# A selective-scan hybrid network on one core: every fourth scan unit takes its input product from GpSimd

## The chip, the cores and the metric

The kernel runs on 1 core of one Trainium2 chip. The metric is the device time of one execution in microseconds (us). Three executions of the kernel before took 7193.72, 7199.61 and 7202.72 us, so the median is 7199.61 us. The five engines of the core are called PE (TensorE), DVE (VectorE), ACT (ScalarE), POOL (GpSimd) and SP (SyncE, which here only issues DMAs). Each has its own queue of instructions and works it off in order.

## The reference

Four images of 1024 positions and 256 channels go through four layers: a convolution and selective-scan block (layer 0, 64 states), a bottleneck convolution (layer 1), graph attention and a mixture of experts (layer 2), and a second selective-scan block with 16 states and another mixture of experts (layer 3). The part that the change touches is the scan. For every channel `d` and state `n` it computes, along the positions:

```python
def step(h, inp):
    xt, dtt, Bt, Ct = inp
    dA = jnp.exp(dtt[:, :, None] * A)
    h = dA * h + (dtt * xt)[:, :, None] * Bt[:, None, :]
    y = jnp.einsum('bdn,bn->bd', h, Ct)
    return (h, y)
```

There are 512 channels, so layer 0 has 512 x 64 such recurrences for each image and layer 3 has 512 x 16.

## The kernel before, in words

**Units.** One unit is a 128 x 1024 f32 tile: 128 recurrences (2 channels with 64 states, or 8 channels with 16 states) on the partitions, 1024 positions along the row. `scans` (L336) lists 1280 of them. The order of the eight scans is fixed by `SCANS` (L31): images 0, 1, 2 of layer 0 (units 0 to 767), images 0 and 1 of layer 3 (768 to 895), image 3 of layer 0 (896 to 1151), and images 2 and 3 of layer 3 (1152 to 1279).

**What a unit does.** `load` (L382) has SP broadcast the rows of `dt` from DRAM over the states into a tile `dA`: two DMAs of 256 KB in layer 0, eight of 64 KB in layer 3. It is called three units ahead, and `dA` has four buffers. `first` (L397), one unit ahead, has PE repeat `dt*u` over the states with two bf16 matmuls into the PSUM tile `ps_rep` (two buffers), and has ACT turn `dA` into the decay exp(A dt) in place. DVE then multiplies `ps_rep` by the row tile of B in place and runs the recurrence with `tensor_tensor_scan` into `h` (five buffers). POOL multiplies `h` by the row tile of C. `pair` (L415) has PE sum two units over the states into `ps_y`.

**What stands beside the units.** All other work belongs to stages (`STAGES`, L33): `front` of an image (what comes before scan 0), `middle` (what follows scan 0 up to the inputs of the image's layer 3 scan: layer 1, attention, experts and `front3`), and `last` (after scan 3: the second expert layer and the output). `front(0)` runs before the first unit and `last(3)` after the last one. The other stages are generators that yield after each small step, and `run` (L490) calls such steps between the units.

**What sets the order.** The scans and the stages run under a manual schedule: instructions stand in each engine's queue in the order in which `run` emits them. `run` keeps a planner's clock for each engine. A wrapper (`Metered`, L88) adds to it a fixed cost for every instruction: for GpSimd's `tensor_tensor` 2.3 us for 1000 columns plus 0.06, for VectorE's 1.18 plus 0.06, for the scan 2.23. After each half of a unit, `run` lets stages advance by at most two steps, and only as long as no clock is ahead of VectorE's:

```python
now = clock["vector"]
for e in clock:
    clock[e] = max(clock[e], now - LAG)
for _ in range(TICKS):
    if max(clock.values()) > clock["vector"] + LEAD or self.advance() is None:
        break
```

`LEAD` is 0, `LAG` is 4 us and `TICKS` is 2. Stages start in the order of `STAGES`, one at a time, as soon as the scan that they wait for is done.

**Where the order is forced.** Twelve units (`AHEAD`) before a scan begins, `chunk` (L356) calls `need` (L465). If the stage that prepares this scan is not finished, `need` advances stages until it is, with no unit in between, and sets all the clocks to the latest one. After the last unit, `run` works off what is left of the stages. In the kernel before, one long stretch is forced: most of `middle(3)`, before the scan of image 3 of layer 3.

**Scatter.** Between the first 64 units POOL also issues one indirect DMA for each unit (`scatter`, L975), which builds the attention mask.

**`steps`** (L527), called at the end of `front` and of `front3`, computes `dt` and `dt*u`, writes `dt` to DRAM, splits `dt*u` into three bf16 parts for PE's repetition, and writes these to DRAM as well. It works on eight items of 128 x 512, with four POOL instructions for each.

Of the kernel before, what the change touches and what calls it, by code (L numbers as in the profile page):

```python
# [7 lines left out]
F32 = mybir.dt.float32  # L8
BF16 = mybir.dt.bfloat16
I32 = mybir.dt.int32  # L10
AF = mybir.ActivationFunctionType
ALU = mybir.AluOpType
# [4 lines left out]
P = 128  # L17
NB = 4
L = 1024
# [16 lines left out]
    ("last", 1, (3, 1)), ("last", 2, (3, 2)),  # L36
)
SAFE = 40.0
AHEAD = 12


# [83 lines left out]
class Hybrid:  # L125
# [41 lines left out]
    def pipe(self, items, *steps, cost=1.0):  # L167

        items = list(items)
        for tick in range(len(items) + len(steps) - 1):  # L170
            for s in reversed(range(len(steps))):
                if 0 <= tick - s < len(items):
                    steps[s](items[tick - s])
            yield cost if tick < len(items) else 0.5
# [126 lines left out]
    def scan_setup(self, stage, psum, name, n):  # L301
# [18 lines left out]
        for s in range(3):  # L320
# [6 lines left out]
        nc.vector.tensor_reduce(  # L327
            mine, self.ident.rearrange("p (g n) -> p g n", n=n), AX.X, ALU.add
        )
# [6 lines left out]
    def scans(self, mp, psum):  # L336

        nc = self.nc
        units = []
        for scan in SCANS:
            G = P // self.states[scan[0]]
            units += [
                (scan, d, c, i, j)
                for d in range(DC) for c in range(2) for i in range(32 // G) for j in range(2)  # L350
            ]
        chunks, rows = {}, {}
        state = {}
        y = None

        def chunk(k):  # L356

            if k >= len(units):
                return
            scan, d, c, i, j = units[k]  # L360
            if (c, i, j) != (0, 0, 0):
                return
            n = self.states[scan[0]]
            if d == 0:
                self.need(scan)
                bct = self.mem["bc", *scan]
                pair = []
                for t in range(2):
                    x = mp.tile([P, L], F32, tag=f"rows{t}", name=f"rows{t}", bufs=2)
                    for g in range(P // n):  # L370
                        nc.sync.dma_start(x[g * n : (g + 1) * n, :], bct[t * n : (t + 1) * n, :])
                    pair.append(x)
                rows[scan] = pair
            S = mp.tile([3 * 32, 4, L], BF16, tag="S", name="S", bufs=2)
            for s in range(3):
                nc.sync.dma_start(
                    S[32 * s : 32 * s + 32, :, :],
                    self.mem["parts", *scan, d][s].rearrange("(j p) t -> p j t", p=32),
                )
            chunks[scan, d] = S  # L380

        def load(k):  # L382
            if k >= len(units):
                return
            scan, d, c, i, j = units[k]
            n = self.states[scan[0]]
            G = P // n
            a = mp.tile([P, L], F32, tag="dA", name="dA", bufs=4)
            for g in range(G):
                r = 64 * c + 32 * j + G * i + g  # L390
                nc.sync.dma_start(
                    a[g * n : (g + 1) * n, :],
                    self.mem["dt", *scan, d][r : r + 1, :].to_broadcast([n, L]),
                )
            state[k] = a

        def first(k):  # L397
            if k >= len(units):
                return
            scan, d, c, i, j = units[k]  # L400
            A, spread, _ = self.tables[scan[0]]
            G = P // self.states[scan[0]]
            ps = psum.tile([P, L], F32, tag="x", name="ps_rep", bufs=2)
            for g in range(2):
                cols = slice(g * 512, (g + 1) * 512)
                nc.tensor.matmul(
                    ps[:, cols], lhsT=spread[:, i, :], rhs=chunks[scan, d][:, 2 * c + j, cols],
                    start=True, stop=True,
                )
            a = state.pop(k)  # L410
            col = (d * P + 64 * c + 32 * j) // G + i
            nc.scalar.activation(a, a, AF.Exp, scale=A[:, col : col + 1])
            state[k] = (a, ps)

        def pair(k):  # L415

            nonlocal y
            scan, d, c, i, j = units[k]
            n = self.states[scan[0]]
            per = 32 * n // P  # L420
            collect = self.tables[scan[0]][2]
            if i == 0:
                y = psum.tile([P, 512], F32, tag="y", name="ps_y", bufs=1)
            h = [state.pop(k - 1), state.pop(k)]
            for g in range(2):
                for j in range(2):
                    at = 32 * (2 * g + j)
                    nc.tensor.matmul(
                        y[at : at + 32, :], lhsT=collect[:, i, :],
                        rhs=h[j][:, g * 512 : (g + 1) * 512],  # L430
                        start=(i == 0), stop=(i == per - 1), tile_position=(0, at),
                    )
            if i == per - 1:
                yo = mp.tile([P, 512], F32, tag="yo", name="yo", bufs=2)
                nc.scalar.copy(yo, y)
                to = self.keep(("y", *scan, d, c), [64, L])
                for g in range(2):
                    nc.sync.dma_start(to[:, g * 512 : (g + 1) * 512], yo[64 * g : 64 * g + 64, :])
                if d == DC - 1 and c == 1:
                    self.done.add(scan)  # L440

        for k in range(AHEAD):
            chunk(k)
        for k in range(3):
            load(k)
        first(0)
        for k in range(len(units) + 4):
            chunk(k + AHEAD)
            load(k + 3)
            first(k + 1)  # L450
            if k < len(units):
                a, inp = state.pop(k)
                B, Cm = rows[units[k][0]]
                nc.vector.tensor_tensor(inp, inp, B, ALU.mult)
            yield
            if k < len(units):
                h = mp.tile([P, L], F32, tag="h", name="h", bufs=5)
                nc.vector.tensor_tensor_scan(h, a, inp, 0.0, ALU.mult, ALU.add)
                nc.gpsimd.tensor_tensor(h, h, Cm, ALU.mult)
                state[k] = h  # L460
            if k % 2 == 1 and 2 <= k < len(units) + 2:
                pair(k - 2)
            yield
# [63 lines left out]
    def steps(self, fp, key, w, src, chunks, bias, u):  # L527


        nc = self.nc  # L530
        for d in range(DC):
            self.keep(("dt", *key, d), [P, L])
            self.keep(("parts", *key, d), [3, P, L], BF16)
        got = {}

        def tile2(tag, bufs):
            return fp.tile([P, 512], F32, tag="sp_" + tag, name="sp_" + tag, bufs=bufs)
# [23 lines left out]
        def split(item):  # L561
            d, g = item
            r, _, _, x = got[item]
            nc.sync.dma_start(self.mem["dt", *key, d][:, g * 512 : (g + 1) * 512], r)
            X = fp.tile([P, 3, 512], BF16, tag="parts", name="parts", bufs=3)
            rest = tile2("x", 2)
            nc.scalar.copy(X[:, 0, :], x)
            nc.vector.tensor_tensor(rest, x, X[:, 0, :], ALU.subtract)
            nc.scalar.copy(X[:, 1, :], rest)
            got[item] = rest, X  # L570

        def low(item):
            rest, X = got[item]
            nc.gpsimd.tensor_tensor(X[:, 2, :], rest, X[:, 1, :], ALU.subtract)

        def store(item):
# [7 lines left out]

        yield from self.pipe(
            [(d, g) for d in range(DC) for g in range(2)], project, add, split, low, store, cost=3.0
        )

# [517 lines left out]
    def shift(self, fp, qT, kT, mT):  # L1106
# [28 lines left out]

        nc.vector.tensor_scalar(most[:, 0:1], most[:, 0:1], SAFE * SAFE, None, ALU.is_lt)
        nc.vector.tensor_scalar(most[:, 0:1], most[:, 0:1], -1.0, 1.0, ALU.mult, ALU.add)
# [583 lines left out]
```

## Time and profile before

| what | value |
|---|---|
| median of 3 executions | 7199.61 us |
| the profiled execution | 7197.44 us, of which the profile's span is 7195.7 us |
| DVE busy | 5221.8 us (73%) |
| PE busy | 5436.2 us (76%) |
| POOL busy | 3649.9 us (51%) |
| ACT busy | 3287.1 us (46%) |
| first scan starts, last scan ends | 317.9 us, 6780.2 us |
| DMA | 939.01 MB, mean 130 GB/s |

The profile is of one execution; its own time is 1.7 us more than its span. A busy share is a mean over stretches of very different kinds, so the stretches have to be told apart: before the first scan, while units run, the one stretch in which a stage is forced and no unit runs, and after the last scan. A line that names L120 is of the wrapper that meters instructions; its tile name tells what it is: `h<-dA,ps_rep` is the scan, `ps_rep<-ps_rep,rows` the product with B, `h<-h,rows` the product with C, `dA<-dA` the decay.

### The profile page before, as it was taken

How to read it: one execution, taken by the hardware profiler on the slowest of the kernel's cores; microseconds unless marked ns; L12 is line 12 of the kernel's file. 1: busy time of each engine (PE TensorE's matmuls, PEld its weight loads, DVE VectorE, ACT ScalarE, POOL GpSimd, SP SyncE). 2: the span in 40 equal slices, each digit the busy share in tenths (PEclk: the TensorE clock that was granted, in tenths of full speed). 3: DMA queues.
4: the chain of work that ended last, by engine and by line, in shares of the span. 5: the costliest groups of instructions: out<-in, count | busy, mean ns of one | idle time of the engine just before them, and what ended most of it. 6: DMA issues, size and time to landing. Idle time of an engine off the chain costs nothing. (4 is left out here: it accounts for less than half of the span.)

```text
span 7195.7 us, 66163 instructions
## 1 busy us (share of the span) xinstructions
PE 5436.2 (76%) x20431; PEld 2208.0 (31%) x20516; DVE 5221.8 (73%) x4477; ACT 3287.1 (46%) x4024; POOL 3649.9 (51%) x1801
## 2 busy tenths in 40 slices
PE   7185876578798568879557889859889777866979
PEld 3020221132242022234113224315444322523556
DVE  2888898878898987889887778889888710237611
ACT  4164665234466334456523446636556332243411
POOL 1287677555557655545755455665555510045300
PEclk8585876579898578979657888969989889876989
DMA  2356665654455664446565545666656610135421
GB/s 81 79 141 163 162 176 161 168 136 120 112 153 159 163 160 125 119 121 174 150 169 133 131 123 143 171 166 159 181 137 164 167 40 1 48 96 154 120 62 32
DMA packets 395051, 939.01 MB, mean 130 GB/s; under 512 B 83268, under 2 KB 165776, under 8 KB 393040
## 3 DMA queue, kind: packets, MB, share of 16 engines
q1 hardware_dynamic: 392512, 932.10, 48.8%
q8 instruction: 172, 2.82, 0.2%
q0 software_dynamic: 2128, 2.13, 0.2%
q14 instruction: 239, 1.96, 0.1%
HBM read 844.17 MB, written 93.95 MB: 130 GB/s over the span
## 5 line engine op out<-in xcount | busy, mean ns | idle before, releaser
L120 POOL TENSOR_TENSOR h<-h,rows 128x1024 f32<-128x1024 f32 x1280 | 3025.5, 2366 | 2208.9 <-DVE h L120 2019.3
L120 DVE TENSOR_TENSOR_SCAN h<-dA,ps_rep 128x1024 f32<-128x1024 f32 x1280 | 2925.2, 2285 | 342.1 <-ACT dA L120 122.3
L120 DVE TENSOR_TENSOR ps_rep<-ps_rep,rows 128x1024 f32<-128x1024 f32 x1280 | 1551.8, 1212 | 270.8 <-PE ps_rep L120 254.5
L120 ACT ACTIVATE dA<-dA,A_L_conv_A_log 128x1024 f32<-128x1024 f32 x1024 | 1156.4, 1146 | 972.4 <-DMA dA<-dt 815.2
L120 PE MATMUL ps_rep<-S,spread_L_conv_A_log 96*128 96x512 bf16 x2048 | 779.2, 471 | 995.8 <-DVE h L120 796.7
L120 PE MATMUL ps_y<-h,collect_L_conv_A_log 128*32 128x512 f32 x4096 | 768.8, 771 | 88.0 <-POOL h L120 84.2
L120 PEld LDWEIGHTS <-spread_L_conv_A_log 96*128 96x128 bf16 x2048 | 159.3, 104 | 1817.3 <-DVE h L120 1370.2
L120 PE MATMUL ps_h<-xTm,we 128*128 128x512 f32 x1280 | 597.9, 611 | 26.0 <-ACT h_m L120 26.0
L120 PE MATMUL ps_e<-we,h_m 128*128 128x256 f32 x2560 | 591.8, 383 | 10.7 <-ACT h_m L120 8.4
L120 ACT ACTIVATE p<-ps_sc 128x512 f32<-128x512 f32 x512 | 277.8, 594 | 580.3 <-PE ps_sc L120 423.5
L120 ACT ACT_TABLE_LOAD x356 | 456.7, 1283 | 184.7 <-DMA dA<-dt 126.1
L120 PEld LDWEIGHTS ps_e<-we,h_m 128*128 128x128 f32 x2560 | 484.3, 191 | 136.8 <-issue 24.8
L120 ACT ACTIVATE dA<-dA,A_L_attn_A_log 128x1024 f32<-128x1024 f32 x256 | 292.5, 1148 | 415.3 <-DMA dA<-dt 380.0
L120 PE MATMUL ps_at<-p,v 128*32 128x512 f32 x1024 | 364.4, 630 | 66.1 <-ACT p L120 58.1
L120 PE MATMUL ps_rep<-S,spread_L_attn_A_log 96*128 96x512 bf16 x512 | 186.9, 453 | 220.9 <-DVE h L120 195.8
L120 PEld LDWEIGHTS ps_h<-xTm,we 128*128 128x128 f32 x1280 | 247.0, 196 | 312.7 <-issue 241.1
L120 ACT ACTIVATE h_m<-ps_h,cols 128x512 f32<-128x512 f32 x320 | 209.6, 685 | 278.0 <-PE ps_h L120 276.6
L120 DVE SCALAR_TENSOR_TENSOR tb<-ps_e,cw,tb 128x256 f32<-128x256 f32 x448 | 192.5, 473 | 191.0 <-PE ps_e L120 190.3
L120 PE MATMUL ps_sc<-qT,kT 32*128 32x512 f32 x1024 | 304.2, 669 | 7.9 <-issue 7.9
L120 PE MATMUL ps_at<-p,ones 128*32 128x512 f32 x1024 | 281.5, 630 | 0.0
L120 DVE RECIPROCAL sums<-sums 128x512 f32<-128x512 f32 x16 | 53.6, 3353 | 303.3 <-ACT sums L120 303.3
L120 PEld LDWEIGHTS ps_y<-h,collect_L_conv_A_log 128*32 128x32 f32 x4096 | 98.1, 120 | 444.6 <-issue 225.8
(406 smaller groups left out, 5695.2 us busy)
## 6 DMA issues: line engine op xcount, KB each, us to landing
dA<-dt SPq DMA_DIRECT2D x2048, 256.0 KB
dA<-dt SPq DMA_DIRECT2D x2048, 64.0 KB
we<-in_L_ffn_W_dram SPq DMA_DIRECT2D x64, 512.0 KB
parts<-parts SPq DMA_DIRECT2D x64, 384.0 KB
S<-parts SPq DMA_DIRECT2D x96, 256.0 KB
dt<-sp_r SPq DMA_DIRECT2D x64, 256.0 KB
y<-yo SPq DMA_DIRECT2D x128, 128.0 KB
y_back<-y SPq DMA_DIRECT2D x64, 256.0 KB
```

What stands on the lines that cost most here:

```text
L120: return got(*args, **kw)
```

## The change

For every fourth unit (the last of each four, `pooled`), four things differ. The values of `dt*u` are also written to DRAM (`dtu`, in `steps`). SP broadcasts their rows over the states into a new SBUF tile `inp` with two buffers (`early`, called five units ahead, with as many DMAs as `load` has). POOL multiplies `inp` by B (`product`, called two units ahead), in place of PE's two matmuls and DVE's product. ACT writes the decay into the PSUM tile in place of `dA`, so that the scan again reads one operand from PSUM and one from SBUF. The other three of four units are as before.

```diff
+TURN = 4
...
-        state = {}
+        state, given = {}, {}
...
+        def pooled(k):
+            return k % TURN == TURN - 1
+
+        def early(k):
+
+            if k >= len(units) or not pooled(k):
+                return
+            scan, d, c, i, j = units[k]
+            n = self.states[scan[0]]
+            G = P // n
+            inp = mp.tile([P, L], F32, tag="inp", name="inp", bufs=2)
+            for g in range(G):
+                r = 64 * c + 32 * j + G * i + g
+                nc.sync.dma_start(
+                    inp[g * n : (g + 1) * n, :],
+                    self.mem["dtu", *scan, d][r : r + 1, :].to_broadcast([n, L]),
+                )
+            given[k] = inp
+
+        def product(k):
+            if k < len(units) and pooled(k):
+                inp = given[k]
+                nc.gpsimd.tensor_tensor(inp, inp, rows[units[k][0]][0], ALU.mult)
+
...
+            if pooled(k):
+                col = (d * P + 64 * c + 32 * j) // G + i
+                nc.scalar.activation(ps, state.pop(k), AF.Exp, scale=A[:, col : col + 1])
+                state[k] = (ps, given.pop(k))
+                return
...
+        for k in range(5):
+            early(k)
...
             chunk(k + AHEAD)
+            early(k + 5)
             load(k + 3)
+            product(k + 2)
             first(k + 1)
...
-                nc.vector.tensor_tensor(inp, inp, B, ALU.mult)
+                if not pooled(k):
+                    nc.vector.tensor_tensor(inp, inp, B, ALU.mult)
...
+            self.keep(("dtu", *key, d), [P, L])
...
+            nc.sync.dma_start(self.mem["dtu", *key, d][:, g * 512 : (g + 1) * 512], x)
```

The planner's constants are left as they are. Its clocks count the new POOL product and no longer count the removed DVE product and PE matmuls.

## The prediction

> **What bounds the kernel now.** I read the table of stretches first: the busy time of each engine from the span's start, in the order PE, PEld, DVE, ACT, POOL, then the granted clock, the DMA share and GB/s.
>
> ```profile
> 1213.00:1384.00 171.00, 93.93 (x288) 11.15 (x288) 160.90 (x96) 53.78 (x48) 111.09 (x48) 0.50 0.63 161
> 318.00:5786.00 5468.00, 4180.26 (x16015) 1569.11 (x16084) 4636.23 (x3565) 2750.02 (x3253) 3316.94 (x1598) 0.79 0.57 151
> 5786.00:6409.00 623.00, 496.39 (x1862) 215.51 (x1877) 83.14 (x196) 202.56 (x334) 70.75 (x57) 0.90 0.09 29
> 6409.00:6780.00 371.00, 257.65 (x956) 115.80 (x955) 286.75 (x229) 163.72 (x171) 191.91 (x88) 0.75 0.59 153
> 6780.00:7195.00 415.00, 372.03 (x1316) 252.16 (x1312) 58.65 (x150) 75.66 (x114) 17.08 (x13) 0.93 0.16 48
> ```
>
> Row 1 holds units with nothing beside them: DVE is busy 160.90 of 171 us, so there it is the bound. Row 3 is the forced middle(3): PE works alone and DVE has 83 of 623 us. Row 5 is the end of last(2) and all of last(3). The units, rows 2 and 4, take 5468 + 371 = 5839 us. Then the costliest groups, and DVE in a stretch without side work:
>
> ```profile
> L120 POOL TENSOR_TENSOR h<-h,rows 128x1024 f32<-128x1024 f32 x1280 | 3025.5, 2366 | 2208.9 <-DVE h L120 2019.3
> L120 DVE TENSOR_TENSOR_SCAN h<-dA,ps_rep 128x1024 f32<-128x1024 f32 x1280 | 2925.2, 2285 | 342.1 <-ACT dA L120 122.3
> L120 DVE TENSOR_TENSOR ps_rep<-ps_rep,rows 128x1024 f32<-128x1024 f32 x1280 | 1551.8, 1212 | 270.8 <-PE ps_rep L120 254.5
> ```
>
> ```profile
> 2402.61 2.29 DVE L120 TENSOR_TENSOR_SCAN h<-dA,ps_rep 128x1024 f32<-128x1024 f32 x1 [0.19 <-issue]
> 2404.81 1.21 DVE L120 TENSOR_TENSOR ps_rep<-ps_rep,rows 128x1024 f32<-128x1024 f32 x1
> 2406.21 2.29 DVE L120 TENSOR_TENSOR_SCAN h<-dA,ps_rep 128x1024 f32<-128x1024 f32 x1 [0.19 <-issue]
> ```
>
> A unit alone takes 2406.21 - 2402.61 = 3.60 us. With side work the mean is 5839/1280 = 4.56 us. So 5839 - 1280 x 3.60 = 1231 us of the units' time is what the side work adds, and in return it hides nearly all of front(1) to last(1).
>
> **Local effect of the change.** Four units now hold three products on DVE, not four. A pooled scan starts when the one before it ends, so four units take 3 x 3.60 + 2.3 = 13.1 us on DVE, or 3.28 a unit, not 3.60. POOL gets five instructions of 2.366 where it had four, 11.8 of 13.1 us. ACT's exponential keeps its 1.15 us (at half this length ACT's rows take 602 ns into PSUM and 597 to 630 into SBUF). PE loses 640 of 2560 bf16 matmuls of 0.46 us, about 300 us spread over all the units. The pooled scan is not in this trace. It has one operand in each memory, as now, so I take 2.285 us; I see nothing that makes it shorter, and the upper end is the factor by which DVE's product of 1024 columns grows when all is in SBUF (y_back 1665 against 1212 ns): 0.85 x 320 = 270 us.
>
> New waits: ACT's exponential of a pooled unit waits until the scan two units back frees the PSUM tile, and ACT's side work queues behind it. That scan ends 3.5 us before the result is needed, and PE's matmuls wait at this place now. POOL's product waits for the `inp` transfer, issued three units earlier, and the C product of the unit before queues behind it; POOL is then 1.1 us late, catches up within four units, and `h` has five buffers. I cost both at nothing in bare units; where front's POOL work comes between, it is in the pace that I take below.
>
> Alone this is 320 x 1.3 = 416 us less. It can't be had as it stands, because **the planner moves the side work**. By its own costs four units are 3 x (1.27 + 2.28) + 2.28 = 12.94 us on VectorE and 5 x 2.415 = 12.08 us on GpSimd. That leaves 0.215 us of GpSimd a unit for stages, or 275 us in 1280 units; before it was 3.55 - 2.415 = 1.14 us a unit. What the stages want of POOL is 3650 busy less 3026 for h, less 65 for the scatter, 45 in front(0) and 15 in last(3): 500 us. The 64 scatter DMAs, at 1.0 us each, come first and eat the room of some 300 units. So about half the side work finds no place beside the units. It is then forced by `need`, or left to the end, where nothing hides it. The order in which the built program's instructions stand says the same and gives the places. Before, only middle(3) (ahead of unit 1204) is forced. Now five things stand with no unit between them: all of front(1) before unit 244; 104 of 128 expert matmul entries and front3 of middle(0) before unit 756; middle(1) from its attention on before 820; all of last(0) but its start and all of middle(3) before 1204; and the experts of last(1), all of last(2) and last(3) after the last unit.
>
> **Forced stretches, by what the same work took alone in this trace.** front(0) from its first statistics (37.6 us) to its last store (209.4) took 172: front(1) 175. In row 3 the experts took 6161 to 6274, front3 6274 to 6410: 104/128 x 113 + 136 = 228. Middle(1) lacks 22 us of row 3's 623: 600. last(3) ran 6893 to 7189, 296 us; last(0) has its first 25 us done, 272; middle(3) is row 3's 623 and back0 with layer 1, which I put at 110 from their instructions (between 80 and 135): 1005 together. Sum **2008 us, where 623 stood**. The tail: last(1) from its experts' routing 250, last(2) 296, last(3) 296 and 3 of turnover: **845 where 415 stood**.
>
> **Units.** Stretches, with the pace of each:
> - 0 to 64: POOL is the bound. 5/4 x 2.366 + 1.01 (indirect DMA) = 3.97, and 4.57 with the 0.6 that each of these waited: 4.4 x 64 = 280.
> - 64 to 244, bare: 3.28 and 0.04 of margin: 3.32 x 180 = 598.
> - 244 to 568, front(2) and front(3) thinly spread: now 62 units with a front take 34 to 39 us over 3.60 each; POOL is near its limit, so I take 3.61: 1170.
> - 568 to 756, back0, layer 1 and attention of middle(0): attention is PE's (4.84 a unit now, 4.5 with fewer matmuls): 780.
> - 820 to 1204: 896 to 1152 hold middle(2), 4.07 a unit, 1042; its layer 3 units stand in the next line.
> - 756 to 820 and all other layer 3 units are **SP's**:
>
> ```profile
> 6736.84 14.93 SPq L391 DMA_DIRECT2D dA<-dt  x32
> ```
>
> 32 issues in 14.93 us are 0.467 each: 8 a unit 3.73 us, already at DVE's pace; with `early` 10 a unit, 4.7. These are 285 (756 to 820), 357 and 244 (820 to 896, 1152 to 1204), and 357 (1204 to 1280).
>
> Units together: 280 + 598 + 1170 + 780 + 1042 + 285 + 357 + 244 + 357 = 5113, that is **726 less than 5839**. DMA: five transfers of 512 KB in 13.1 us are 200 GB/s. This row shows a burst for one unit:
>
> ```profile
> 2402.40:2404.40 2.00, 1.85 (x8) 0.12 (x8) 1.81 (x2) 1.15 (x1) 1.40 (x1) 0.50 0.90 246
> ```
>
> So 246 GB/s is had, and loads are issued about 10 us before their scan and land in 4.6. I cost them at nothing; if 181 GB/s, the highest slice of the page, were the limit, a bare unit would take 3.62.
>
> The Trainium skill ("SBUF — State Buffer", section "Door 1: The DMA port swizzle") speaks against this: 64 partitions reach only 8 of 16 ports, 196 GB/s, and two such transfers at once gain 6%. By it five transfers would take 12.6 to 13.4 us, level with DVE, and the sum would grow by up to 60 us. The 246 GB/s above are over its figure, so the row is taken.
>
> The `dtu` stores (64 issues of about 0.4 us on SP, mostly where SP is idle) and one `early` ahead of the first load cost 4 us at the start: 322. The sum is 322 + 5113 + 2008 + 845 = 8288 us for the profiled execution; its 7197.44 us stands 2 us below the median, so **8290 us**, 15% slower.
>
> **Rivals.**
> - DVE's freed time decides and the order costs nothing: 7197 - 416 = 6780, faster. For it: DVE's 160.90 of 171 us. Against: the forced stretches hold none of the pooled work. It decides only if they shrink to today's 623. 2%; no change at all 1%.
> - The same order, but units nearer their floors: layer 3 units at 3.3 since SP catches up in the forced stretches (-1.4 x 250 = -350), fronts at 3.4 (-70), middle(2) at 3.7 (-95): 7775. 12%.
> - Transfers or POOL bound all bare units: +0.34 x 830 = 280, or scans slower out of PSUM, +270: 8570, both 8840. 15%.
> - My forecast: 70%.
>
> Slower in 97, faster by over 0.2% in 2, within it in 1 of 100 (0.2% is about what a measurement of this kernel can tell from no change). The range, 7960 to 8600, takes in the unknown sizes of back0, of POOL's waits (50 us each) and of the pace under side work (0.25 us on 900 units), half of the way to the lower rival and the upper one's single price.
>
> **What would show it.** DVE's longest gaps ahead of scans 244, 756, 820 and 1204, of about 175, 230, 600 and 1000 us; three expert stages after the last scan; POOL's group of 320 products at 2.37 us; bare units at 13.1 us for four; layer 3 units at 4.7 with SP issuing without a break. It is wrong if those gaps are filled with scans, if a pooled scan takes over 2.4 us, or if DVE waits for POOL's product or the `inp` transfer in the bare units.

## The result and the profile after

The kernel with the change takes **8502.96 us** (median of four executions, 8495.25 to 8509.75), the kernel before 7200.54 us (four executions). The ratio is 1.181, with a 95% interval of 1.179 to 1.183. The prediction was 8290 us in a range of 7960 to 8600: the direction and the range hold, and the prediction is 213 us too low.

The profiled execution of after took 8495.25 us and its span is 8493.5 us. The page cuts the span into 40 slices of 212 us; these are the busy tenths of DVE and POOL, and the traffic of the DMAs.

```profile
DVE  3768974899898876272115677989541011561111
POOL 2388975898897775262005666779630000550000
GB/s 93 102 134 199 212 168 138 210 219 218 208 226 190 180 157 121 118 152 70 5 48 161 153 166 147 175 204 213 173 97 59 16 7 60 162 146 36 58 56 35
```

Read the first two rows as a map. DVE at 8 or 9 is a place where units run at DVE's speed. Where DVE and POOL fall together to 0 to 2 in the second half, no unit runs: slices 17, 19 to 21, 31 to 34 and the last four. The table of stretches gives these places their edges, which are the ends and starts of the scans around DVE's long gaps. The columns are window and length, then busy us of PE, PEld, DVE, ACT and POOL, the granted clock, the DMA share and GB/s.

```profile
314.00:627.00 313.00, 163.84 (x342) 17.81 (x342) 200.31 (x112) 76.11 (x68) 247.08 (x142) 0.50 0.63 147
627.00:1228.00 601.00, 297.93 (x995) 36.01 (x990) 557.64 (x316) 207.35 (x185) 528.11 (x230) 0.53 0.88 204
1228.00:1388.00 160.00, 110.75 (x246) 44.55 (x243) 17.76 (x41) 76.39 (x136) 41.53 (x34) 0.79 0.17 62
3346.00:3566.00 220.00, 184.91 (x526) 99.02 (x523) 40.42 (x93) 86.36 (x129) 41.05 (x33) 0.91 0.21 72
3897.00:4502.00 605.00, 477.62 (x1788) 206.66 (x1805) 83.08 (x196) 195.09 (x321) 65.78 (x53) 0.89 0.11 36
4502.00:4918.00 416.00, 193.62 (x670) 65.33 (x669) 264.46 (x193) 113.19 (x127) 242.16 (x112) 0.63 0.60 158
6261.00:7243.00 982.00, 813.09 (x2944) 427.56 (x2961) 149.31 (x368) 275.06 (x446) 81.75 (x66) 0.89 0.13 40
7656.00:8493.00 837.00, 753.35 (x2602) 504.84 (x2600) 116.73 (x295) 156.75 (x235) 31.77 (x25) 0.92 0.16 47
```

Row 1 is units 0 to 64. Rows 3, 4, 5 and 7 are the four gaps ahead of scans 244, 756, 820 and 1204, row 6 is units 820 to 896 of layer 3, and row 8 is the tail. In the four gaps and the tail DVE is idle for four fifths of the time or more, and PE works on stages. Row 2 is a stretch of units with hardly any side work: DVE is busy 557.64 of 601 us. Rows 1 and 6 are units in which no engine is busy throughout; what holds them comes below.

The sum of after and the sum of before, each against its own span:

| part | before | after | difference |
|---|---|---|---|
| to the first scan | 318 | 315 | -3 |
| forced, no unit running | 623 | 1966 | +1343 |
| 1280 units | 5839 | 5376 | -463 |
| after the last scan | 415 | 837 | +422 |
| span | 7195.7 | 8493.5 | +1298 |

The costliest groups of after, from the page: busy time and mean ns, then the idle time before them and what ended most of it.

```profile
L121 POOL TENSOR_TENSOR h<-h,rows 128x1024 f32<-128x1024 f32 x1280 | 3006.1, 2358 | 1248.9 <-DVE h L121 1140.3
L121 DVE TENSOR_TENSOR_SCAN h<-dA,ps_rep 128x1024 f32<-128x1024 f32 x960 | 2193.9, 2285 | 448.3 <-ACT dA L121 212.0
L121 DVE TENSOR_TENSOR ps_rep<-ps_rep,rows 128x1024 f32<-128x1024 f32 x960 | 1161.0, 1209 | 165.0 <-PE ps_rep L121 164.0
L121 DVE TENSOR_TENSOR_SCAN h<-ps_rep,inp 128x1024 f32<-128x1024 f32 x320 | 727.5, 2274 | 404.6 <-POOL inp L121 187.8
L121 POOL TENSOR_TENSOR inp<-inp,rows 128x1024 f32<-128x1024 f32 x320 | 754.9, 2359 | 5.8 <-issue 4.5
```

The pooled scan (fourth line) takes 2274 ns against 2285 of the others, and POOL's new product costs what its old one does. DVE has lost 320 products, 1161.0 us where 1551.8 stood. So the change does what it says, piece by piece, and DVE's busy time falls from 5221.8 to 4834.1 us. The new waits show in the last columns: 187.8 us of the idle time before pooled scans ends with POOL's product.

### The profile page after: what moved, and what is told of

It reads as the page before. It is cut to its first block, busy times and chain, and to the rows that moved or that the text cites. A ratio compares the mean times of both kernels' runs of the same rounds, so it can differ in the third digit from the quotient of the medians.

```text
span 8493.5 us, 66636 instructions
## 1 busy us (share of the span) xinstructions
PE 5575.9 (66%) x19800; PEld 2163.3 (25%) x19876; DVE 4834.1 (57%) x4157; ACT 2978.5 (35%) x3766; POOL 4361.8 (51%) x2121
## 5 line engine op out<-in xcount | busy, mean ns | idle before, releaser
L121 DVE TENSOR_TENSOR_SCAN h<-dA,ps_rep 128x1024 f32<-128x1024 f32 x960 | 2193.9, 2285 | 448.3 <-ACT dA L121 212.0
L121 PE MATMUL ps_rep<-S,spread_L_conv_A_log 96*128 96x512 bf16 x1536 | 663.7, 527 | 1373.9 <-DVE h L121 1233.0
L121 DVE TENSOR_TENSOR ps_rep<-ps_rep,rows 128x1024 f32<-128x1024 f32 x960 | 1161.0, 1209 | 165.0 <-PE ps_rep L121 164.0
L121 ACT ACTIVATE dA<-dA,A_L_conv_A_log 128x1024 f32<-128x1024 f32 x768 | 876.8, 1147 | 1023.6 <-DMA dA<-dt 1016.9
L121 PE MATMUL ps_y<-h,collect_L_conv_A_log 128*32 128x512 f32 x4096 | 933.5, 887 | 206.6 <-POOL h L121 186.1
L121 DVE TENSOR_TENSOR_SCAN h<-ps_rep,inp 128x1024 f32<-128x1024 f32 x320 | 727.5, 2274 | 404.6 <-POOL inp L121 187.8
L121 POOL TENSOR_TENSOR inp<-inp,rows 128x1024 f32<-128x1024 f32 x320 | 754.9, 2359 | 5.8 <-issue 4.5
L121 ACT ACTIVATE ps_rep<-dA,A_L_conv_A_log 128x1024 f32<-128x1024 f32 x256 | 286.0, 1117 | 570.7 <-DVE h L121 432.6
L121 ACT ACTIVATE dA<-dA,A_L_attn_A_log 128x1024 f32<-128x1024 f32 x192 | 220.2, 1148 | 725.9 <-DMA dA<-dt 606.3
L121 POOL TENSOR_TENSOR sp_l<-sp_l,sp_e 128x512 f32<-128x512 f32 x56 | 70.8, 1264 | 757.4 <-DVE sp_e L121 712.9
L121 POOL TENSOR_TENSOR raw<-raw,sums 128x512 f32<-128x512 f32 x16 | 20.2, 1263 | 604.6 <-DVE sums L121 604.6
```

What stands on the lines that cost most here:

```text
L121: return got(*args, **kw)
```

## The experiments

**The theory on record** has two halves. (A) The order: POOL's new product takes POOL's slack away in the planner's books, the stages then find no place beside the units, and what is forced or left over runs alone. (B) The units: the pooled work itself saves some time where DVE bounds, and costs time where POOL (the scatter) or SP (layer 3) bounds. The main rival gives the loss to the pooled work itself: contention, scans out of PSUM, transfers, or waits.

**e1_ledger: all the pooled work, with the planner charged as before.** The side work then stands between the same units as in the kernel before.

```diff
-                nc.gpsimd.tensor_tensor(inp, inp, rows[units[k][0]][0], ALU.mult)
+                nc.what.gpsimd.tensor_tensor(inp, inp, rows[units[k][0]][0], ALU.mult)
...
             if pooled(k):
+                self.clock["tensor"] += 2 * matmul_us(ps[:, :512], lhsT=spread[:, i, :])
...
-                if not pooled(k):
+                if pooled(k):
+                    self.clock["vector"] += by_columns(1.18, 0.06)(inp)
+                else:
                     nc.vector.tensor_tensor(inp, inp, B, ALU.mult)
```

(`nc.what` is the engine without the planner's meter.)

> The changed kernel with the planner's clocks charged as in the kernel before (the product on VectorE, the two matmuls on TensorE, nothing for GpSimd), so that the side work stands between the same units as before the change; all the pooled work is done. Theory A (the order is the cause): only middle(3) is forced again, about 620 us, the tail is 415, and the units gain 0.25 us in layer 0 and lose some 0.4 in layer 3: 7000 to 7250 us. Theory B (GpSimd, SP and the transfers are really overloaded, and the planner only says so): 8000 us or more, with DVE waiting for POOL's products or for transfers in the units.

Measured: 7367.77 us (7358.67 to 7374.96), ratio 1.0219 (1.0198 to 1.0240). The gap before scan 1204 is 631 us and the tail 420, as before the change; the other gaps are gone. So 1135 of the 1302 us by which after is longer went with the planner's charges alone. But the expected gain on top did not come: the pooled work costs 164 us net in the order of the kernel before. Theory A holds here, and the net of half B had the wrong sign.

**e2_order: the work of the kernel before, in the order of after.** Nothing is computed by POOL; the planner is only told so.

```diff
+        def pooled(k):
+            return k % TURN == TURN - 1
+        def product(k):
+            if k < len(units) and pooled(k):
+                self.clock["gpsimd"] += 2.3e-3 * L + 0.06
...
-                nc.vector.tensor_tensor(inp, inp, B, ALU.mult)
+                (nc.what if pooled(k) else nc).vector.tensor_tensor(inp, inp, B, ALU.mult)
```

(The two matmuls of a pooled unit go past the meter in the same way.)

> The kernel before, with nothing of the pooled work, but with the planner's clocks charged as in the changed kernel, so that the side work stands where the change puts it. Theory A: the five forced stretches (about 160, 220, 605, 980 us and a tail of 840) are all there, and bare units take 3.6 us: 8250 to 8500 us. Theory B: about 7200 us, as before.

Measured: 8467.05 us, ratio 1.1744 (1.1717 to 1.1771). Two of its gaps, in the table of stretches of e2_order:

```profile
3987.00:4596.00 609.00, 485.10 (x1804) 207.67 (x1805) 83.25 (x196) 195.32 (x321) 65.85 (x53) 0.88 0.10 31
6297.00:7277.00 980.00, 810.68 (x2960) 426.32 (x2959) 149.70 (x368) 275.62 (x446) 82.07 (x66) 0.89 0.12 37
```

They are rows 5 and 7 of after, to within 4 us, and nothing of the pooled work exists in this kernel. The tail is 836.5 us against 837.0. This is the clean proof of (A): **1263 us come with the order alone**, against 1302 for the whole change. In that order, e2's 1280 units take 5347 us (its span less the same parts) and after's 5376: with the pooled work added, the units as a whole gain nothing. That sum hides two halves of one size, which the table of units in the next section shows: in layer 0's units from 64 on after is 237 us shorter than e2, in units 0 to 64 it is 59 us longer, and in layer 3's stretches 207.

**e3_ledger_l0: e1 with layer 0 pooled only.** This takes the `inp` transfers of layer 3 off SP.

```diff
-            return k % TURN == TURN - 1
+            return k % TURN == TURN - 1 and units[k][0][0] == 0
```

> As e1_ledger, but only units of layer 0 are pooled; layer 3 units are as in the kernel before. If SP's ten issues a unit are what makes layer 3 units long, these fall from about 5.4 to about 5.1 us and the time is 80 to 150 us below e1_ledger: 6900 to 7130. If they are not, it is within 30 us of e1_ledger or above it, since 64 DVE products come back.

Measured: 7201.85 us (ten executions), ratio 0.9996 (0.9984 to 1.0008), the same as before. The step below e1, 166 us, is a little more than the 80 to 150 expected; the range of 6900 to 7130 is missed because it stood on the e1 that was expected. Layer 3's 64 pooled units so cost 166 us, 2.6 us each. The 256 of layer 0 cancel out to nothing, which the stretches below take apart.

**e4_actq: e1 with layer 3's `inp` transfers issued by ACT.**

```diff
-                nc.sync.dma_start(
+                (nc.sync if G == 2 else nc.scalar).dma_start(
```

> As e1_ledger, but in layer 3 the eight transfers of dt*u for a pooled unit are issued by ACT, not by SP. If it is the issuing on SP, layer 3 units fall to the level of e3_ledger_l0 or below: 60 to 150 us less than e1_ledger. If it is the transfers themselves, no change within 30 us; if ACT's queue suffers from the issuing, longer.

Measured: 7462.34 us, ratio 1.0347 (1.0327 to 1.0366), 95 us slower than e1: the third case of its expectation. An issue takes 406 ns of ACT's queue (the mean of 112 issues in units 832 to 890), ahead of the exponentials that DVE waits for. This run does not tell whether SP's issues were what bound e1.

**e8_twoissues: e1 with two DMAs for a layer 3 `inp` tile in place of eight.** Bytes and partitions written stay, the number of issues falls from 8 to 2. The layer 3 scans then get wrong inputs.

```diff
-            for g in range(G):
-                r = 64 * c + 32 * j + G * i + g
+            for g in range(2):
...
-                    inp[g * n : (g + 1) * n, :],
-                    self.mem["dtu", *scan, d][r : r + 1, :].to_broadcast([n, L]),
+                    inp[g * 64 : (g + 1) * 64, :],
+                    self.mem["dtu", *scan, d][r : r + 1, :].to_broadcast([64, L]),
```

> As e1_ledger, but dt*u of a pooled layer 3 unit comes by two transfers of 256 KB (two channels' rows over 64 partitions each, in place of eight channels over 16, so the layer 3 scans have wrong inputs) and not by eight of 64 KB: the same bytes with six issues fewer. If the issues on SP make layer 3 units long, the time falls by 80 to 150 us towards e3_ledger_l0; if the bytes or the waits of the pooled unit do, by less than 40.

Measured: 7255.4 us, ratio 1.0083 (1.0068 to 1.0099), 112 us faster than e1 (101 us, when each is taken against the executions of the kernel before that were timed beside it: 7193.10 us here, 7204.01 for e1). SP's queue in e1 and then in e8, four units of layer 3 each (start, length, line, count of issues):

```profile
4205.06 3.61 SPq L411 DMA_DIRECT2D inp<-dtu  x8
4208.77 15.78 SPq L392 DMA_DIRECT2D dA<-dt  x32
```

```profile
4153.38 1.18 SPq L411 DMA_DIRECT2D inp<-dtu  x2
4154.66 15.47 SPq L392 DMA_DIRECT2D dA<-dt  x32
```

In these rows SP issues all but without a break, so the 40 issues of e1 take 19.4 us for four units and the 34 of e8 16.7. The layer 3 stretches of e8 sum to 1316 us, those of e1 to 1406, those of before to 1260. **So 90 of layer 3's 146 us come from the six issues a pooled unit that e8 saves, and not from the bytes.** That the bytes could flow faster shows in after too: 204 GB/s in units 64 to 244 (row 2) and 158 in layer 3 (row 6), with the same bytes for a unit. Why the other 56 us stay was not tried.

**e5_late: e3 without the units below 212; e6_bare: only three bare stretches pooled** (units 212 to 259, 460 to 507 and 716 to 763, which have no side work beside them).

```diff
-            return k % TURN == TURN - 1 and units[k][0][0] == 0
+            return k % TURN == TURN - 1 and units[k][0][0] == 0 and k >= 212
```

```diff
+            return k % TURN == TURN - 1 and units[k][0][0] == 0 and any(a <= k < a + 48 for a in (212, 460, 716))
```

> As e3_ledger_l0, but units before 212 (the scatter and the three fronts) are not pooled. If POOL's queue there (scatter, front and product) is what ate the gain, the 68 + 7 + 7 us by which units 0 to 208 were longer in e3_ledger_l0 come back: 7110 to 7150 us, 0.7 to 1.3% faster than before. If something else did, 7190 or more.

> As e5_late, but only the units that have no side work beside them (212 to 259, 460 to 507, 716 to 763) are pooled. If a pooled unit beside side work gives nothing, this is within 15 us of e5_late; if it gives its 0.3 us, it is 40 us or more above it. By the bare stretches of e3_ledger_l0 (14 + 17 + 17 us) 7150 to 7165 us.

Measured: e5 7124.65 us, ratio 0.9907 (0.9889 to 0.9925); e6 7147.21 us, ratio 0.9939 (0.9924 to 0.9954). Both are faster than the kernel before, by under 1% but clear of the interval, and they show where the pooled work gains and loses. e6 lies 23 us above e5, between the two cases of its expectation; 19 us of that are in units 971 to 1151. Stretches between scan starts, in us, all with before's order, so that the columns compare like with like:

| units | beside them | before | e1 | e3 | e5 | e9 |
|---|---|---|---|---|---|---|
| 0 to 83 | scatter, front(1) | 373 | 439 | 441 | 375 | 374 |
| 84 to 208 | fronts | 524 | 536 | 538 | 523 | 523 |
| 209 to 255 | nothing | 171 | 157 | 157 | 155 | 150 |
| 290 to 394 | attention | 525 | 527 | 527 | 527 | 522 |
| 459 to 511 | nothing | 192 | 175 | 175 | 175 | 172 |
| 715 to 766 | nothing | 190 | 173 | 174 | 173 | 173 |
| 971 to 1151 | middle(2), front(3) | 793 | 774 | 780 | 775 | 784 |
| layer 3 (767 to 895, 1152 to 1203, 1216 to 1279) | middle, last | 1260 | 1406 | 1264 | 1257 | 1270 |

(e9 is the last experiment below.) The bare stretches gain 48 us together in e3, which is as much as e6 gains as a whole (46). Units 0 to 208 lose 82, which is why e3 as a whole shows nothing. The rest of the side work shows no gain for the most part. The first row in the table of stretches of before and of e3:

```profile
318.00:691.00 373.00, 262.29 (x736) 68.77 (x736) 310.56 (x207) 190.09 (x238) 304.14 (x183) 0.74 0.60 153
```

```profile
320.00:761.00 441.00, 276.91 (x692) 68.12 (x692) 291.59 (x186) 190.13 (x238) 348.04 (x202) 0.67 0.65 158
```

POOL already had 304 of 373 us there. The product adds 44 us of POOL's work, and the stretch becomes 68 us longer, while DVE gives up 19 us of work that it did not lack time for. The other 24 us of the 68 are POOL's too: its idle time before the 64 indirect DMAs, most of which ends when an earlier indirect DMA has landed, grows from 39.0 to 62.6 us. Before, then e3:

```profile
L120 POOL DMA_INDIRECT mask_dram<-zero,where x64 | 64.8, 1012 | 39.0 <-DMA mask_dram<-zero,where 31.8 <-issue 5.3 <-DVE ps_rep L120 0.8
```

```profile
L121 POOL DMA_INDIRECT mask_dram<-zero,where x64 | 64.4, 1006 | 62.6 <-DMA mask_dram<-zero,where 49.5 <-issue 4.4 <-PE ps_y L121 3.8
```

e2, which has no pooled work, has 40.8 us before these 64, so the growth comes with the pooled work; by which way was not tried. DVE feels POOL's queue in a line of e3's waits in this stretch (total us, number, longest):

```profile
DVE h L121 <- POOL inp L420: 90.5, 15, 12.7
```

The pooled scan waits 90.5 us for POOL's product, six us each time, because the product stands in POOL's queue behind the scatter, front(1) and the C products. And here is the attention stretch (units 290 to 394), before and e3:

```profile
1540.00:2070.00 530.00, 446.90 (x2034) 158.27 (x2056) 424.07 (x337) 253.65 (x332) 280.86 (x131) 0.84 0.47 121
```

```profile
1627.00:2154.00 527.00, 442.78 (x2013) 159.81 (x2012) 394.94 (x311) 255.28 (x332) 333.54 (x152) 0.84 0.60 146
```

DVE is relieved of 29 us and the stretch keeps its length: DVE was not the bound. PE has 443 to 447 of some 530 us, the fullest of the engines; which chain through PE holds the stretch was not separated.

**e7_sbuf: e3 with the decay in SBUF**, as the three other units have it. The pooled scan then has both operands in SBUF.

```diff
-                nc.scalar.activation(ps, state.pop(k), AF.Exp, scale=A[:, col : col + 1])
-                state[k] = (ps, given.pop(k))
+                a = state.pop(k)
+                nc.scalar.activation(a, a, AF.Exp, scale=A[:, col : col + 1])
+                state[k] = (a, given.pop(k))
```

(A pooled unit then takes no PSUM tile at all.)

> As e3_ledger_l0, but the decay of a pooled unit stays in the SBUF tile, so that its scan reads both operands from SBUF and ACT waits for no PSUM tile. If ACT's wait for PSUM is what takes the gain in the stretches with side work, these get shorter and the time falls by 40 us or more. If two SBUF operands slow the scan beside GpSimd, pooled scans take more than 2.29 us, up to the 1.37 times that bounded it in the prediction (3.1 us, 256 units, 200 us more).

Measured: 7324.26 us, ratio 1.0193 (1.0164 to 1.0221), 122 us slower than e3 (133 us, each against the executions of before that were timed beside it). The group of pooled scans, first in e7 and then in e3:

```profile
L121 DVE TENSOR_TENSOR_SCAN h<-dA,inp 128x1024 f32<-128x1024 f32 x256 | 802.3, 3134 | 254.0 <-POOL inp L420 120.3 <-ACT dA L121 91.3 <-DMA dA<-dt 26.3
```

```profile
L121 DVE TENSOR_TENSOR_SCAN h<-ps_rep,inp 128x1024 f32<-128x1024 f32 x256 | 583.5, 2279 | 253.4 <-ACT ps_rep L121 118.1 <-POOL inp L420 107.4 <-issue 7.2
```

The same scan takes 3134 ns on average instead of 2279, and up to 9177 ns for one. The idle time before it stays (254.0 and 253.4 us), so the instruction itself is slower while POOL works: in e7's trace the 26 pooled scans that overlap no POOL instruction take 2267 to 2293 ns, the 230 others 3230 on average. This is what writing the decay to PSUM buys: 219 us of scan time in 256 units. The Trainium skill ("SBUF — State Buffer", section "Who interferes with whom") states that a VectorE instruction with two SBUF inputs contends with a GpSimd instruction that reads SBUF, and that one with at most one SBUF input, outside the 2-port performance modes, does not; both halves agree with these two rows. POOL's C product slows as well, from 2367 to 2524 ns.

The kernel before had shown this already. `y_back` is a VectorE operation with two inputs in SBUF; here are two of them (1256 and then 3362 ns) and the POOL product beside them:

```profile
1412.70 4.54 DVE L120 SCALAR_TENSOR_TENSOR y_back<-u_back,cols,y_back 128x1024 f32<-128x1024 f32 x2
1412.92 3.23 POOL L120 TENSOR_TENSOR h<-h,rows 128x1024 f32<-128x1024 f32 x1 [7.52 <-DVE h L120]
```

The product started while the first ran, and took 3.23 us in place of 2.37. The second started while the product ran, and ended only 1.1 us after it.

**e9_turn3: e5 with every third unit pooled; e10_turn8: after with every eighth, planner charged honestly.**

```diff
-TURN = 4
+TURN = 3
```

```diff
-TURN = 4
+TURN = 8
```

> As e5_late, but every third unit is pooled (layer 0, from unit 212 on). In bare units DVE then needs (2 x 3.60 + 2.3)/3 = 3.17 us a unit and POOL 4/3 x 2.36 = 3.15: if nothing else binds, some 150 bare units gain 0.13 us each, 10 to 20 us below e5_late (7105 to 7115). The transfers rise to about 221 GB/s in bare units, near the highest slice that the changed kernel showed (226): if they bind, it is equal to e5_late or above.

> The changed kernel as it is, with its honest planner's costs, but every eighth unit pooled. By the planner's costs eight units then leave 27.1 - 21.7 = 5.4 us of GpSimd, 0.67 a unit or 860 us in all, more than the 565 that stages and scatter want. Theory A: most side work finds its place again; by the built order only the stretch ahead of unit 1204 grows (all of middle(3) and 200 of 256 expert entries of last(1), about 910 us), the tail is about 425: 7350 to 7550 us. If the pooled units themselves were the cause of the 1300 us, half as many would cost half: about 7850.

Measured: e9 7110.11 us (7098.6 to 7120.77), ratio 0.9866 (0.9843 to 0.9889), the best version of this study, 1.3% faster than the kernel before. e10 7393.28 us, ratio 1.0268 (1.0245 to 1.0291), inside what theory A expected: half as many pooled units, and the forced time shrinks to one gap of 871 us with a tail of 434. The stages before scans 244, 756 and 820 find their place again. A bare stretch of e9 in its table of stretches:

```profile
1205.00:1365.00 160.00, 84.16 (x268) 11.38 (x268) 152.17 (x86) 57.21 (x52) 154.61 (x69) 0.61 1.01 240
```

DVE has 152 and POOL 155 of 160 us, and the DMA engines are busy throughout (1.01): three resources are all but full at once, at 3.18 us a unit in units 209 to 255. Pooling still more units there would find none of them free.

## Why the prediction was right, and what was mis-sized

**The order and the forced stretches: right.** The five places were forecast from the order of the instructions and the sizes from the same work's time alone in before.

| place | predicted | after |
|---|---|---|
| before scan 244 | 175 | 160 |
| before scan 756 | 228 | 220 |
| before scan 820 | 600 | 605 |
| before scan 1204 | 1005 | 982 |
| after the last scan | 845 | 837 |

The forced sum was 2008 and is 1966; the largest miss is 23 us. Experiment e2 shows that the order is the cause, and not only a coincidence of sums: the same gaps stand without any pooled work.

**The units: 5113 forecast, 5376 measured.** This is more than the whole miss; the gaps, the tail and the start, 57 us shorter together than forecast, give some of it back. The forecast lies 234 us below the 5347 of e2, which has the order without the pooled work, so it counted on a net gain from the pooled work; measured is 29 us of loss.

| units | predicted | after | miss | e2 |
|---|---|---|---|---|
| 0 to 64 | 280 | 313 | +33 | 254 |
| 64 to 244 | 598 | 601 | +3 | 666 |
| 244 to 568 | 1170 | 1145 | -25 | 1242 |
| 568 to 756 | 780 | 814 | +34 | 840 |
| 756 to 820, 820 to 896, 1152 to 1204, 1204 to 1280 | 1243 | 1417 | +174 | 1210 |
| 896 to 1152 | 1042 | 1087 | +45 | 1135 |

**Layer 3: the largest mis-sized term is "with `early` 10 a unit, 4.7".** That SP's issues lengthen it is right, as e8 shows, and so is the price of 0.467 us for an issue. Two batches of after on SP's queue:

```profile
4642.98 18.07 SPq L392 DMA_DIRECT2D dA<-dt  x32
7405.12 14.72 SPq L392 DMA_DIRECT2D dA<-dt  x32
```

The second has 32 issues at 0.46 us. The first has the same distance of 0.46 us between most starts, and one wait of SP of 2.9 us for a scan (at 4654.6). What the term left out is the rest of the queue. In units 832 to 896 SP issued 674 DMAs, 10.5 a unit and not 10, since the `S` loads and the `y` stores go the same way. At 0.463 us these are 312 of 338 us, and the other 26 are waits and slower issues (single ones took up to 1.9 us), where the term had SP "without a break". The measured pace is 5.28 us a unit here and 5.20 in units 1216 to 1280. The second omission is that units start slowly after these gaps: the first 12 took 5.4, 6.6 and 6.7 us each (from 756, 820 and 1204), together some 70 us of the 174. In e2 they took 5.6, 6.0 and 6.2, so this is not the pooled work's; its cause was not tried. The rival in which SP catches up during the forced stretches, with 3.3 us a unit, fails: loads are emitted three units ahead into four buffers, so SP has nothing of theirs to issue there.

**Units 0 to 64: the bound was right (POOL), the wait too small.** 4.88 a unit against 4.4. The sum's own terms gave 4.57 with the 0.6 us that each indirect DMA waited in before, and 4.4 was taken. In after that wait is 0.99 us (61.6 for 62 in the stretch 314 to 627):

```profile
L121 POOL DMA_INDIRECT mask_dram<-zero,where x62 | 62.1, 1002 | 61.6 <-DMA mask_dram<-zero,where 54.4 <-issue 3.0 <-PE ps_y L121 2.2
```

With it the same sum gives 4.96. POOL is busy for 247.1 us and waits for 61.6 of the stretch's 313. What DVE sees of it stands in its waits: 11 of 16 pooled scans waited for POOL, 6.8 us each.

```profile
DVE h L121 <- POOL inp L121: 74.4, 11, 12.6
```

"I cost both at nothing in bare units; where front's POOL work comes between, it is in the pace that I take" put this in a pace that was too low.

**Units 568 to 756 and 896 to 1152: "4.5 with fewer matmuls" came out, but not by fewer matmuls.** The attention of middle(0) took 299 us in after (2914 to 3213, first to last matmul into `ps_sc`, the scores) and 4.53 us a unit in units 664 to 729. But in e2, where no matmul has gone, it took 301 us (3040 to 3341), with PE busy for 274.4 us against 260.9. In the order of before the attention stretch also keeps its 5.0 us a unit in e1, e3 and e5. So the matmuls that leave are not what holds attention, and the agreement of 4.5 with 4.53 is luck. Most of the 34 us missed in 568 to 756 are found behind attention: units 729 to 755 took 5.1 us each, and 5.2 in e2. What holds those, and the 45 us of 896 to 1152, was not separated.

**Bare units: right.** 3.34 a unit in 64 to 244 against 3.32 (3.70 in e2, without the pooled work), the pooled scan at 2274 ns against 2285, and POOL's product at 2359 against 2366. The 1.37 that was the pooled scan's upper end is no property of `y_back`: it is the mean of 16 rows, of which 13 took 1256 to 1285 ns and the three that started beside a running POOL product 3362. That e7's mean is 1.37 times 2285 as well is luck: it is another mixture of fast and slow rows. Two scans in a row, without POOL's product in between being waited for, in DVE's timeline of after:

```profile
904.08 2.29 DVE L121 TENSOR_TENSOR_SCAN h<-dA,ps_rep 128x1024 f32<-128x1024 f32 x1 [0.19 <-ACT ps_rep L121]
906.28 2.27 DVE L121 TENSOR_TENSOR_SCAN h<-ps_rep,inp 128x1024 f32<-128x1024 f32 x1
```

**"Alone this is 320 x 1.3 = 416 us less": wrong.** e1 is this case, and it is 164 us more. The 1.3 us are had only where DVE bounds: in the bare stretches (48 us) and some 20 us in 971 to 1151. Elsewhere in the order of before something else sets the pace, and the gain is zero beside attention, negative beside the scatter and the fronts (79 us) and in layer 3 (146 us). The forecast of after survived this because it priced the stretches one by one, and because the gaps and the tail, 1765 us more than before, outweigh it. The first rival, 6780 us, was out of reach even without the order: e5 and e9, which leave the harmful places out, reach 7125 and 7110.

**The weighed rule.** The prediction took the trace's burst of 246 GB/s for more than the Trainium skill's 196 GB/s for 64 partitions ("SBUF — State Buffer", section "Door 1: The DMA port swizzle") with 6% from a second transfer (same page, section "Can I just issue two DMAs to hit both halves?"), 208 together. Over longer times after does not decide it: 204 GB/s over 601 us of bare units lies below 208. e9 does, narrowly: it moves 240 GB/s over 160 us, and the 130 broadcasts of 256 KB to 64 partitions in this window are 213 GB/s by themselves.

## What to carry to other kernels

When instructions are emitted in an order that a planner computes from costs, an edit that moves work to another engine changes the planner's books too: price the order first, by reading where side work now stands, and try the edit with the books left as they were. Price a relief of the busiest engine stretch by stretch, and apply it only where that engine ends the waits; in this kernel the same edit gains 0.3 us a unit in bare stretches and loses 0.8 a unit where POOL's queue was nearly full already. Count DMA issues like instructions: at about half a microsecond each, ten small ones a unit all but fill a queue that moves the same bytes in two or three with time to spare.

## What the runs showed of the hardware

- A scan of 128 x 1024 f32 with both operands in SBUF took 3134 ns on average and up to 9177 ns beside POOL's products, against 2279 with one operand in PSUM; POOL's C product went from 2367 to 2524 ns (e7 and e3). Where no POOL instruction overlapped such a scan, it took 2267 to 2293 ns (26 in e7).
- SP issued the 64 KB broadcasts of layer 3 at 0.45 us (8 in 3.61) to 0.49 us (32 in 15.78) each in e1, and at 0.46 us (32 in 14.72) in after; two of 256 KB took 1.18 us, 0.59 each (e8). Moved to ACT, an issue held ACT's queue for 406 ns (e4).
- The DMA engines held 240 GB/s for 160 us at a busy share of 1.01, 213 of it broadcasts to 64 partitions each (e9).
- 64 indirect DMAs on POOL had 39.0 us of idle time before them in before, 40.8 in e2 and 62.6 in e3, where the pooled work was added.
- ACT's exponential took 1117 ns into PSUM and 1147 in place in SBUF, so writing the decay to PSUM costs ACT no time in the instruction itself:

```profile
L121 ACT ACTIVATE ps_rep<-dA,A_L_conv_A_log 128x1024 f32<-128x1024 f32 x256 | 286.0, 1117 | 570.7 <-DVE h L121 432.6
L121 ACT ACTIVATE dA<-dA,A_L_conv_A_log 128x1024 f32<-128x1024 f32 x768 | 876.8, 1147 | 1023.6 <-DMA dA<-dt 1016.9
```
